# A graph layer's last group gets an order of its own: wide one-hots two groups sooner, the last quad in halves, normalizations in batches counted from the end

## The chip, the cores and the metric

The kernel runs on one core of one Trainium2 chip. The metric is the device time of the core in microseconds (us). Before the change it was 2016.4 us, the median of three runs (2014.7 to 2017.06). The engines have these short names: PE is TensorE (matmuls; PEld its weight loads), DVE is VectorE, ACT is ScalarE, POOL is GpSimd, and SP is SyncE, which only issues transfers here.

## What is computed

There are 6250 nodes with 128 features and 206250 edges, sorted by their receiver. Each edge gets a weight vector from two small networks, a score per head from the receiver's query, the sender's key and that weight, and adds score times the sender's value to its receiver. Each node's sum is added to its features and normalized.

```python
w  = silu(edge_feats @ rad_W1 + rad_b1) @ rad_W2 + rad_b2
w += silu(chi_scalar @ sph_W1 + sph_b1) @ sph_W2 + sph_b2
q_i = (x @ Wq)[receivers]; k_j = (x @ Wk)[senders]; v_j = (x @ Wv)[senders]
alpha = (q_i * w * k_j).sum per head / sqrt(16) * cutoff
out = segment_sum(alpha * v_j, receivers) / 16
return layernorm(x + out)          # per row, eps 1e-5
```

## The kernel before, in words

**Tiling.** 128 edges make a tile, four tiles a *quad* (512 edges), four quads a *group*. There are 403 quads in 101 groups; the last group, 100, has three. Inside a group the quads go in the order 0, 2, 1, 3, and the list `order` holds all of them. In this text "quad i" is the one at place i of `order`, so group g has quads 4g to 4g+3, and the last group's three are **a** (i = 400), **b** (401) and **c** (402).

**Start.** Keys and values of all nodes are computed and stored as a table in HBM, one row of 1 KB per node. The first ten quads are fed by gathers from `x` instead.

**Gathers.** The sender's rows come by `gathers`: four indirect transfers a quad, issued by POOL (the line of the helper is L125), one for each tile, into a ring of 16 buffers `kv`. They are issued 14 quads ahead, and each waits for a matmul of the quad that PE is at ("no gather ahead of TensorE"). Six quads (65, 130, ... 390) get their rows by 512 single transfers from SP instead (`load_rows`, buffers named `rows`, two of them). This stays as it is.

**A slot of the loop (L641 to L710).** In slot i PE makes the first layers of quad i+2 (L446), the queries at the edges of quad i+1 (`q_at_edges`, L457, into one of two PSUM buffers `pq`) and the second layer of quad i+1 (`weigh`, L488 and L493, into one of two buffers `pw`). ACT makes the two silus of quad i+2 (L478). DVE does `multiply(i+1)` (L500: query times key, which needs the gathered rows), then `scores(i)` (L507, L509, L511) and `messages(i)` (L522). PE later sums the messages of a group by one-hot matrices: `sum_quads` (L533), `part_sums` (ACT, L562), `sum_group` (PE, L567 and L569, which carries the group before along through a `to` matrix made by `place`, L556 and L557), and ACT copies the total (`tot`, L571). The engines work in the order of the program; waits on matmuls are put on certain instructions by hand (`after`, `behind`), so that a wait of DVE or ACT is for PE's current quad.

**The normalization (`statistics`, L573).** Two groups later, in the last slot of a group, DVE adds `x` to the total and takes mean and variance (L579 to L582). Every fourth group the batch is finished: one root on ACT (L585), a reciprocal and a shift on DVE (L587, L589), and the rows on ACT (L592). The batches are groups 0 to 3, 4 to 7, ..., 92 to 95; then 96 and 97 together, 98 alone, and 99 and 100 in the code behind the loop. Root and silu are of different tables on ACT, so that each such batch also has two table loads (rows `ACT_TABLE_LOAD`). The finished rows are written by SP (`write_rows`, L599), one group a slot. Where to is known only at run time, so each write waits for the one before it, and the very last one (L749) too.

**The last group.** It is summed by *wide* one-hots over 128 receivers (`wide_one_hots`, L537: three DVE instructions, the last of them 128x512) instead of `sum_quads`. Before, these lie in buffers of the silus (`act`) and are made in slots 399, 400 and 401. Behind the loop (L711 to L749) the last `sum_group`, the last quad's scores and messages in two halves, and the moments of groups 99 and 100 follow. A flag (`general`) that tells whether a slow general path is needed is loaded into registers of all engines at L696.

The lines at which the ends meet:

```python
messages(q, scores(q, halves[0]), halves[0])     # L729
...
moments(0, tot_of[g - 1])                        # L732: group 99
...
messages(q, alpha, halves[1])                    # L737
...
moments(1, po_of[g])                             # L744: group 100
...
nc.sync.dma_start(out[N - P:, :], y)             # L749
```

Of the kernel before, what the change touches and what calls it, by code (L numbers as in the profile page):

```python
# [24 lines left out]
P = 128  # L25
N = 6250
D = 128
# [31 lines left out]
def gnn_kernel(ctx, tc, x, src, dst, weight, edges, rad_W1, rad_b1, rad_W2, rad_b2,  # L59
# [344 lines left out]
    with tc.tile_pool(name="ps", bufs=1, space=PSUM) as pp:  # L404
# [93 lines left out]
        def multiply(q, mark=None):  # L498
            kq_of[q] = quad_of("kq", 3)
            o = nc.vector.tensor_tensor(kq_of[q], pq_of[q], kv_of[q][:, :, :D], op=OP.mult)  # L500
            if mark is not None:
                after(o, mark)
# [33 lines left out]

        def wide_one_hots(q):  # L537
# [5 lines left out]
            hot_of[q, "wide"] = ep.tile([P, EQ], F32, name="act", bufs=8).rearrange(  # L543
                "p (t r) -> p t r", r=P)
# [7 lines left out]
        def place(g):  # L552

            to = to_of[g] = gp.tile([P, 2, P], F32, name="to")
# [18 lines left out]
        def statistics(g):  # L573
            first = g // LB * LB if g < NG - 3 else g
# [3 lines left out]
            k = g - first + 1  # L578
            nc.vector.tensor_tensor(y0[:, k - 1, :], tot_of[g], x_of[g], op=OP.add)  # L579
            st = gp.tile([P, 6], F32, name="st")  # L580
            nc.vector.bn_stats(st, y0[:, k - 1, :])
            nc.vector.bn_aggr(mv[:, k - 1, :], st)  # L582
            if k == LB or g >= NG - 4:
                sd = gp.tile([P, LB], F32, name="sd")
                nc.scalar.activation(sd[:, :k], mv[:, :k, 1], AF.Sqrt, bias=eps)  # L585
                rs = gp.tile([P, LB], F32, name="rs")
                nc.vector.reciprocal(rs[:, :k], sd[:, :k])  # L587
                shift = gp.tile([P, LB], F32, name="shift")
                nc.vector.scalar_tensor_tensor(shift[:, :k], mv[:, :k, 0], -1.0, rs[:, :k],  # L589
                                               op0=OP.mult, op1=OP.mult)  # L590
                for i in range(k):
                    nc.scalar.activation(y0[:, i, :], y0[:, i, :], AF.Identity,  # L592
                                         scale=rs[:, i:i + 1], bias=shift[:, i:i + 1])
                    written.append((first + i, y0[:, i, :]))
# [46 lines left out]
        for g in range(NG):  # L641
            last = g == NG - 1
            for slot, j in enumerate((0, 2, 1, 3)):
                q = g * NQ + j
                i = g * NQ + slot
                if q >= QUADS:
                    continue
# [3 lines left out]
                if slot == 0 and g + 1 < NG:  # L651
# [3 lines left out]
                if slot == 2 and g + 1 < NG:  # L655
                    turned = make_q(g + 1)
                if 1 <= g:
                    for t in ((), (0, 1), (2, 3))[slot] if last else ((), (0, 1), (2,), (3,))[slot]:
                        mark = sum_quads(g - 1, t)
                if last and slot == 2:  # L660
                    po_of[g] = pp.tile([P, EQ], F32, name="ph", bufs=2)[:, :D]
                    for t in range(QT):
                        sum_wide(order[i - 2], t, start=(t == 0))
                if i + 2 < len(order):
                    first_layers(order[i + 2])
                if i + 1 < len(order):
                    mark = q_at_edges(order[i + 1])
                    marks = weigh(order[i + 1])
                if i + 2 < len(order):
                    silus(order[i + 2], mark, marks)  # L670
# [6 lines left out]
                if i + 1 < len(order):  # L677
                    multiply(order[i + 1], mark)
                    messages(q, scores(q, marks=marks), marks=marks)
# [6 lines left out]
                if slot == 1:  # L686
                    if g + 1 < NG:
# [220 lines left out]
```

## Time and profile before

| what | us |
|---|---|
| median of three runs | 2016.4 |
| the profiled execution's own time | 2016.52 |
| span of the profile (first to last instruction) | 2014.7 |
| busy in the span: PE, DVE, POOL, ACT | 1808.9, 1466.3, 1504.8, 720.1 |
| granted PE clock over the span | 0.92 |

The profiled execution took 2016.52 us, of which 1.8 us lie outside the span. Rows of the timeline give the start in us from the span's start, the duration in us, the engine, the line, the operation, what is written from what, and in brackets the idle time of the engine just before and what ended it. A row can stand for several instructions (the number behind x). Lines such as L500 are lines of the kernel before.

### The profile page before, as it was taken

The page shows a single profiled execution, that of the slowest core. Times are in us where ns is not written, and L with a number is a line of the kernel's source. Part 1 is how long each engine was busy: PE and PEld are TensorE (multiplying, and loading weights), DVE is VectorE, ACT ScalarE, POOL GpSimd, SP SyncE. Part 2 cuts the span into 40 slices and gives each one's busy share as a digit, 9 for nine tenths or more (in the row PEclk, how much of TensorE's full clock was granted, in tenths as well). Part 3 has the DMA queues.
Part 4 walks back from the last instruction along what each step waited for, and adds up shares of the span by engine and source line. Part 5 has one row for each costly group of instructions (what it writes and reads, how often), then busy time and mean ns, then how long its engine had stood idle before and what let it go on. Part 6 is the DMA issues. An engine that isn't in the chain of part 4 may idle for free.

```text
span 2014.7 us, 50499 instructions
## 1 busy us (share of the span) xinstructions
PE 1808.9 (90%) x16012; PEld 1515.0 (75%) x16012; DVE 1466.3 (73%) x3012; ACT 720.1 (36%) x1425; POOL 1504.8 (75%) x1596
## 2 busy tenths in 40 slices
PE   9898888999999988899999988988888999889987
PEld 7787777877887777777777777777777787777776
DVE  6687767878887867677767676777776777767776
ACT  2333333334433423333333233333333343332333
POOL 7777777777777777777777777777777777777774
PEclk9898988999998998998988888999998989899898
DMA  8454545555555555555454555454545555555552
GB/s 311 133 151 141 155 142 152 156 156 155 152 153 148 153 152 144 153 152 152 142 155 143 150 144 153 141 153 141 153 142 151 156 142 151 151 146 150 145 151 73
DMA packets 146414, 304.47 MB, mean 151 GB/s; under 512 B 36716, under 2 KB 79580, under 8 KB 146140
## 3 DMA queue, kind: packets, MB, share of 16 engines
q0 software_dynamic: 75584, 205.62, 36.4%
q1 hardware_dynamic: 69056, 95.15, 14.8%
q8 instruction: 128, 2.10, 0.4%
q14 instruction: 146, 1.20, 0.2%
q10 hardware_dynamic: 1500, 0.40, 0.1%
HBM read 287.58 MB, written 13.46 MB: 149 GB/s over the span
## 4 chain that ended last, share of the span: by engine, by line
PE 51%; DMA 21%; DVE 11%; issue 6%; ACT 4%; SPq 4%; POOL 3%; DVEq 0%; ACTq 0%; POOLq 0%
PE pw L493 25%; DMA kv<-kv_tab,src_i 17%; PE pq L457 10%; PE ph L446 7%; DVE kq L500 4%; PE po L533 3%; DMA feats<-in_edges 3%; SPq L167 3%; PE pw L488 2%; DVE kq L507 2%; DVE side L509 2%; POOL msg L125 2%; ACT y L592 1%; ACT L478 1%; POOL kv L125 1%
## 5 line engine op out<-in xcount | busy, mean ns | idle before, releaser
L125 POOL DMA_INDIRECT kv<-kv_tab,src_i x1548 | 1465.1, 946 | 474.3 <-PE pw L493 183.9
L478 ACT ACTIVATE act<-ph,b 128x512 f32<-128x512 f32 x806 | 518.2, 685 | 1159.8 <-PE pq L457 1126.5
L493 PE MATMUL pw<-w,act 128*128 128x128 f32 x6448 | 912.8, 300 | 0.0
L493 PEld LDWEIGHTS pw<-w,act 128*128 128x128 f32 x6448 | 831.6, 209 | 107.5 <-issue 95.9
L446 PE MATMUL ph<-feats,w 32*128 32x512 f32 x1612 | 495.2, 673 | 53.6 <-DMA feats<-in_edges 29.6
L457 PE MATMUL pq<-q,hotT 32*128 32x128 f32 x3224 | 498.1, 297 | 39.0 <-DVE kq L500 38.8
L500 DVE TENSOR_TENSOR kq<-pq,kv 128x512 f32<-128x512 f32 x397 | 273.1, 688 | 323.7 <-DMA kv<-kv_tab,src_i 169.3
L457 PEld LDWEIGHTS pq<-q,hotT 32*128 32x128 f32 x3224 | 418.6, 199 | 76.5 <-issue 45.1
L509 DVE TENSOR_REDUCE side<-kq 128x32 f32<-128x512 f32 x404 | 280.0, 693 | 42.3 <-PE pw L493 0.9
L522 DVE TENSOR_TENSOR msg<-kv,side 128x512 f32<-128x512 f32 x398 | 273.2, 686 | 44.0 <-DVE side L511 1.4
L507 DVE TENSOR_TENSOR kq<-pw,kq 128x512 f32<-128x512 f32 x404 | 274.2, 679 | 0.0
L446 PEld LDWEIGHTS ph<-feats,w 32*128 32x128 f32 x1612 | 135.5, 192 | 136.9 <-issue 90.3
L488 PE MATMUL pw<-brow,onesb 3*128 3x512 bf16 x403 | 161.6, 401 | 0.3 <-DVE kq L507 0.3
L533 PE MATMUL po<-msg,hot 128*32 128x128 f32 x3200 | 154.7, 290 | 0.0
L567 PE MATMUL pq<-part,to 128*128 128x128 f32 x200 | 45.2, 309 | 76.1 <-DVE kq L500 48.9
L511 DVE TENSOR_TENSOR side<-side,scale 128x32 f32<-128x32 f32 x404 | 80.6, 199 | 42.9 <-DVE side L509 0.9
L432 DVE TENSOR_TENSOR hotT<-relb,side 128x512 f32<-128x512 bf16 x101 | 68.8, 682 | 45.3 <-DMA relb<-rel_lin 45.3
L533 PEld LDWEIGHTS po<-msg,hot 128*32 128x32 f32 x3200 | 70.8, 111 | 39.0 <-issue 6.0
L567 PEld LDWEIGHTS pq<-part,to 128*128 128x128 f32 x200 | 31.3, 197 | 86.7 <-issue 53.8
L437 DVE TENSOR_TENSOR hot<-rel,side 128x512 f32<-128x512 f32 x100 | 66.1, 661 | 0.0
L426 PE MATMUL pq<-wq,xT 128*128 128x128 f32 (+1 forms) x202 | 46.8, 318 | 20.0 <-DVE kq L500 19.6
L426 PEld LDWEIGHTS pq<-wq,xT 128*128 128x128 f32 (+1 forms) x202 | 36.0, 223 | 24.6 <-DVE kq L500 23.8
(113 smaller groups left out, 839.3 us busy)
## 6 DMA issues: line engine op xcount, KB each, us to landing
feats<-in_edges SPq DMA_DIRECT2D x101, 512.0 KB
rows<-kv_tab SPq DMA_DIRECT2D x3072, 1.0 KB
kv<-kv_tab,src_i POOLq DMA_INDIRECT x1548
relb<-rel_lin SPq DMA_DIRECT2D x101, 128.0 KB
x<-in_x SPq DMA_DIRECT2D x101, 64.0 KB
out<-y SPq DMA_DIRECT2D x101, 64.0 KB
kv_tab<-kv SPq DMA_DIRECT2D x12, 512.0 KB
act<-in_x SPq DMA_DIRECT2D x12, 256.0 KB
```

The costliest lines, as they stand in the source:

```text
L125: return nc.gpsimd.indirect_dma_start(out=o, out_offset=None, in_=table, in_offset=bass.IndirectOffsetOnAxis(ap=index, axis=0))
L426: nc.tensor.matmul(pt[:n, :D], xT_of[g][:, :n], wq, start=True, stop=True)
L446: return nc.tensor.matmul(act_of[q, i], w1[r0:r0 + R, :], feats_of[g][r0:r0 + R, c0:c0 + EQ], start=True, stop=True)
L457: o = nc.tensor.matmul(pq_of[q][:, t, :], hotT_of[g][b, t * P:(t + 1) * P], q_of[g][b, :], start=True, stop=True)
L478: o = nc.scalar.activation(act, act_of[q, i], AF.Silu, bias=b1[:, i:i + 1])
L488: nc.tensor.matmul(pw, onesb, brow.rearrange("p t d -> p (t d)"), start=True, stop=False)
L493: o = nc.tensor.matmul(pw[:, t, :], act_of[q, i][:, t * P:(t + 1) * P], w2[:, i, :], start=False, stop=(t == QT - 1 and i == 1))
L500: o = nc.vector.tensor_tensor(kq_of[q], pq_of[q], kv_of[q][:, :, :D], op=OP.mult)
L507: nc.vector.tensor_tensor(m, pw_of[q][:, t, :], m, op=OP.mult)
L509: o = nc.vector.tensor_reduce(alpha, m.rearrange("p t (h e) -> p t h e", e=HD), AX.X, OP.add)
L522: o = nc.vector.tensor_tensor(msg_of[q][:, t, :].rearrange("p t (h e) -> p t h e", e=HD), kv_of[q][:, t, D:].rearrange("p t (h e) -> p t h ...
L533: o = nc.tensor.matmul(po_of[g][j * W:(j + 1) * W, :], hot_of[g][:, j * QT + t, :], msg_of[g * NQ + j][:, t, :], start=(t == 0), stop=(t = ...
```

## The change

It gives the last group an order written out by hand.

- **Loop.** It ends with group 99 (all conditions on the last group go away). The slots of groups 0 to 99 keep their instructions apart from what follows.
- **Wide one-hots.** They are made in slots 392 (a), 394 (b) and 396 (c) instead of 399, 400 and 401, and lie in the two buffers `rows` of the single transfers. `place(100)` goes to slot 398 (with a buffer of its own, `to_end`), `place(99)` to slot 399, the load of `general` from slot 401 to slot 396.
- **Batches of the normalization.** They are counted from the end: group 0 alone, then 1 to 4, ..., 93 to 96; the last batch is finished in slot 395. Groups 97, 98, 99 and 100 are normalized one by one. There are 29 roots instead of 28.
- **Behind the loop.** Silus of c before the root of group 97; `multiply(b)`; scores and messages of a; normalization of 97; then scores and messages of b; moments of 98; then `multiply`, scores and messages of c in two halves, with the normalization of 98 and the moments of 99 between the halves, and the normalization of 99 behind them; then the moments of group 100, its normalization on DVE and the last write.

The diff, cut to its core:

```diff
-        def multiply(q, mark=None):
-            kq_of[q] = quad_of("kq", 3)
-            o = nc.vector.tensor_tensor(kq_of[q], pq_of[q], kv_of[q][:, :, :D], op=OP.mult)
+        def multiply(q, mark=None, t=slice(0, QT)):
+            if t.start == 0:
+                kq_of[q] = quad_of("kq", 3)
+            o = nc.vector.tensor_tensor(kq_of[q][:, t, :], pq_of[q][:, t, :], kv_of[q][:, t, :D],
+                                        op=OP.mult)
...
-            hot_of[q, "wide"] = ep.tile([P, EQ], F32, name="act", bufs=8).rearrange(
-                "p (t r) -> p t r", r=P)
+            k = order[-3:].index(q)
+            if k % 2 == 0:
+                wides.append(quad_of("rows", 2, 2 * D).rearrange("p t (h r) -> p h t r", r=P))
+            hot_of[q, "wide"] = wides[-1][:, k % 2]
...
+        def first_of(g):
+            return max(g - (g - (NG - LB)) % LB, 0)
...
+        def statistics(g):
+            moments(g, tot_of[g])
+            if g < NG - LB and first_of(g + 1) > g:
+                normalize(first_of(g), g + 1, roots(first_of(g), g + 1))
...
-        for g in range(NG):
-            last = g == NG - 1
+        for g in range(NG - 1):
...
+                if g == NG - 3 and slot in (0, 2):
+                    wide_one_hots(order[slot // 2 - 3])
+                if g == NG - 2 and slot == 0:
+                    wide_one_hots(order[-1])
+                    n = nc.values_load(general, min_val=0, max_val=1)
+                if g == NG - 2 and slot == 2:
+                    place(NG - 1)
+                if g == NG - 2 and slot == 3:
+                    place(g)
+        g, (a, b, c) = NG - 1, order[-3:]
+        first_layers(c)
+        mark = q_at_edges(b)
+        marks = weigh(b)
+        turned = sum_group(g - 2)
+        for t in range(QT // 2):
+            sum_quads(g - 1, t)
+        silus(c, mark, marks)
+        sd = roots(g - 3, g - 2)
+        turned()
+        multiply(b, mark)
+        messages(a, scores(a, marks=marks), marks=marks)
+        normalize(g - 3, g - 2, sd)
+        write_rows()
+        mark = q_at_edges(c)
+        marks = weigh(c)
+        for t in range(QT // 2, QT):
+            sum_quads(g - 1, t)
+        po_of[g] = pp.tile([P, EQ], F32, name="ph", bufs=2)[:, :D]
+        for t in range(QT):
+            sum_wide(a, t, start=(t == 0))
+        part_sums(g - 1)
+        turned = sum_group(g - 1)
+        messages(b, scores(b, marks=marks), marks=marks)
+        moments(g - 2, tot_of[g - 2])
+        sd = roots(g - 2, g - 1)
+        turned()
+        for t in range(QT):
+            sum_wide(b, t)
+        nc.tensor.matmul(po_of[g], to_of[g][:, 1, :], tot_of[g - 1], start=False, stop=False)
+        multiply(c, mark, halves[0])
+        messages(c, scores(c, halves[0]), halves[0])
+        for t in range(QT // 2):
+            sum_wide(c, t)
+        normalize(g - 2, g - 1, sd)
+        write_rows()
+        moments(g - 1, tot_of[g - 1])
+        sd = roots(g - 1, g)
+        multiply(c, mark, halves[1])
+        messages(c, scores(c, halves[1]), halves[1])
+        for t in range(QT // 2, QT):
+            sum_wide(c, t, stop=(t == QT - 1))
+        normalize(g - 1, g, sd)
+        write_rows()
+        moments(g, po_of[g])
+        sd = roots(g, g + 1)
...
         nc.sync.dma_start(out[N - P:, :], y)
```

`roots` and `normalize` are the two halves of what `statistics` did at the end of a batch: the root on ACT, and reciprocal, shift and rows.

More of the change, by code (lines that the diff above doesn't have):

```diff
@@ L577, in statistics @@
             y0, mv = y0_of[first]
-            k = g - first + 1
-            nc.vector.tensor_tensor(y0[:, k - 1, :], tot_of[g], x_of[g], op=OP.add)
+            k = g - first
+            nc.vector.tensor_tensor(y0[:, k, :], total, x_of[g], op=OP.add)
             st = gp.tile([P, 6], F32, name="st")
[L581 to L594, printed above, removed]
+            nc.vector.bn_stats(st, y0[:, k, :])
@@ L650, in gnn_kernel @@
                     verdict()
-                if slot == 0 and g + 1 < NG:
+                if slot == 0:
                     turned = turn_q(g + 1)
```

106 lines of the change are left out of this document (42 added, 64 removed).

## The prediction

> **What bounds the kernel now.** I read the groups of instructions first, then the waits of POOL, then POOL's timeline.
>
> ```profile
> span 2014.7 us, 50499 instructions
> ...
> PE 1808.9 (90%) x16012; PEld 1515.0 (75%) x16012; DVE 1466.3 (73%) x3012; ACT 720.1 (36%) x1425; POOL 1504.8 (75%) x1596
> ...
> L125 POOL DMA_INDIRECT kv<-kv_tab,src_i x1548 | 1465.1, 946 | 474.3 <-PE pw L493 183.9
> ```
>
> ```profile
> POOL kv L125 <- PE pw L493: 183.9, 595, 2.8
> ```
>
> ```profile
> 53.84 0.95 POOL L125 DMA_INDIRECT kv<-kv_tab,src_i  x1 [0.31 <-issue]
> ...
> 77.09 0.95 POOL L125 DMA_INDIRECT kv<-kv_tab,src_i  x1 [2.79 <-PE pw L493]
> ```
>
> ```profile
> 1987.09 0.95 POOL L125 DMA_INDIRECT kv<-kv_tab,src_i  x1 [0.30 <-issue]
> ...
> 1992.08 0.95 POOL L125 DMA_INDIRECT kv<-kv_tab,src_i  x1 [0.30 <-issue]
> ```
>
> POOL looks 75% busy and PE 90%, yet POOL is the bound. 1548 gathers of 0.946 us, with 474.3/1548 = 0.306 us ahead of each, make a period of 1.25 us; 1548 x 1.252 is 1938 us, and from the first row (53.84) to the end of the last (1993.03) there are 1939 us. The waits put down to PE are 183.9/595 = 0.309 us each, the same 0.3 us that stands ahead of every gather, so this is POOL's own gap and no wait. One wait was real, the longest: 2.79 us at 77.09. A quad's four gathers take 5.00 us, and the last gathers of b and c start at 1987.09 and 1992.08. Nothing that the change does on other engines shortens this chain. What it can change is the tail: 2014.7 - 1993.0 = 21.7 us behind the last gather, and how soon the other engines are ready for it.
>
> **The tail before.** DVE, then PE and ACT, then SP's queue:
>
> ```profile
> 1985.32 0.69 DVE L500 TENSOR_TENSOR kq<-pq,kv 128x512 f32<-128x512 f32 x1 [1.15 <-DMA kv<-kv_tab,src_i]
> ...
> 1989.61 0.17 DVE L587 RECIPROCAL rs<-sd 128x2 f32<-128x2 f32 x1 [0.36 <-ACT sd L585]
> ...
> 1989.89 0.16 DVE L541 CAST d<-dst_i 128x4 f32<-128x4 int32 x1
> ...
> 1991.24 0.69 DVE L500 TENSOR_TENSOR kq<-pq,kv 128x512 f32<-128x512 f32 x1
> 1991.85 0.68 DVE L507 TENSOR_TENSOR kq<-pw,kq 128x512 f32<-128x512 f32 x1
> ...
> 1994.34 0.16 DVE L541 CAST d<-dst_i 128x4 f32<-128x4 int32 x1
> ...
> 1995.93 0.68 DVE L500 TENSOR_TENSOR kq<-pq,kv 128x512 f32<-128x512 f32 x1
> ...
> 2001.81 0.42 DVE L507 TENSOR_TENSOR kq<-pw,kq 128x256 f32<-128x256 f32 x1
> 2002.26 0.43 DVE L509 TENSOR_REDUCE side<-kq 128x16 f32<-128x256 f32 x1
> ...
> 2002.94 0.42 DVE L522 TENSOR_TENSOR msg<-kv,side 128x256 f32<-128x256 f32 x1
> 2004.26 0.29 DVE L722 TENSOR_TENSOR y<-tot,x 128x128 f32<-128x128 f32 x1 [0.90 <-ACT tot L571]
> ...
> 2005.01 0.39 DVE L507 TENSOR_TENSOR kq<-pw,kq 128x256 f32<-128x256 f32 x1
> ...
> 2006.25 0.42 DVE L522 TENSOR_TENSOR msg<-kv,side 128x256 f32<-128x256 f32 x1
> ...
> 2008.87 0.34 DVE L747 TENSOR_SCALAR y<-y,mv,rs 128x128 f32<-128x128 f32 x1
> ```
>
> ```profile
> 1991.99 1.43 PE L457 MATMUL pq<-q,hotT 32*128 32x128 f32 x5 [1.94 <-DVE kq L500]
> ...
> 1998.71 1.21 PE L549 MATMUL ph<-msg,act 128*128 128x128 f32 x8
> 2002.63 0.80 PE L567 MATMUL pq<-part,to 128*128 128x128 f32 x2 [2.71 <-ACT part L562]
> ```
>
> ```profile
> 1990.01 0.88 ACT L592 ACTIVATE y<-y,shift,rs 128x128 f32<-128x128 f32 x2 [0.43 <-DVE shift L589]
> ...
> 2003.95 0.28 ACT L571 ACTIVATE tot<-pq 128x128 f32<-128x128 f32 x1 [1.37 <-PE pq L569]
> ...
> 2006.42 0.49 ACT L740 ACTIVATE y<-y,shift,rs 128x128 f32<-128x128 f32 x1 [0.94 <-DVE shift L735]
> ```
>
> ```profile
> 2006.94 0.33 SPq L599 DMA_DIRECT2D out<-y  x1
> 2010.18 0.34 SPq L749 DMA_DIRECT2D out<-y  x1
> ```
>
> ```profile
> SPq L599 <- DMA out<-y: 4.1, 3, 1.9
> ...
> SPq L749 <- DMA out<-y: 2.8, 1, 2.8
> ```
>
> DVE does kq of a, b and c at 1985.32, 1991.24 and 1995.93. From kq of b to the last messages (2006.25) it needs 15.01 us, in which it also makes the wide one-hots of b and c and waits 0.90 us for the total of group 99. Two things set the end. DVE finishes the last row at 2008.87 + 0.34 = 2009.21, but SP issues the last write only at 2010.18: it waits 2.8 us for the write of group 99, issued at 2006.94, to land. So the end hangs on group 99's rows (2006.42 on ACT), which hang on DVE's queue.
>
> **The change, part by part.** The loop's slots keep their instructions, so POOL's 1548 gathers and the place of the last one stay: cost nothing, by the saturated period above.
>
> *Wide one-hots, `place`, `general` earlier.* About 1.6 us of DVE (1994.34 to 1995.93 holds one quad's wide one-hot and a `place`) go from each of the slots 399 to 401 into 392 to 398, where DVE waits for gathers and PE. There they lie under waits like the 1.15 us at 1985.32; if that cover is gone, 1.6 us are late in one slot. The buffers `rows` were last read in slot 390 by DVE itself, so nothing waits for them. The load of `general` stands in PE's queue behind the second layer of quad 397:
>
> ```profile
> L696 PEldq TENSOR_LOAD <-general x1: 491/491/491, 1994.0 to 1994.0; - x1
> ```
>
> Here it ran at 1994.0, while matmuls already issued kept PE busy (the windows below show PE busy all 3.40 us from 1992.0): nothing, and 0.5 us in one slot if PE has nothing in hand.
>
> *The batch 93 to 96 in slot 395.* Before, a batch of four ended in slot 391, and this is what followed:
>
> ```profile
> 1957.60 0.69 DVE L500 TENSOR_TENSOR kq<-pq,kv 128x512 f32<-128x512 f32 x1 [2.91 <-PE pq L457]
> ...
> 1963.10 0.69 DVE L500 TENSOR_TENSOR kq<-pq,kv 128x512 f32<-128x512 f32 x1 [1.04 <-PE pq L457]
> ...
> 1971.12 0.68 DVE L500 TENSOR_TENSOR kq<-pq,kv 128x512 f32<-128x512 f32 x1
> ```
>
> These are the kq of quads 394, 395 and 397. Last gathers start 5.00 us apart back from 1987.09 (quad 401), so theirs at 1952.1, 1957.1 and 1967.1. So kq lies 5.5, 6.0 and 4.0 us behind the gather, against 3.23 us where DVE waits for the landing (quad 400: 1985.32, its gather at 1982.09). DVE waits for PE (the brackets), since root, rows and table loads hold up the silus that PE needs, and six quads behind the batch it is not all made up. In the changed kernel the same comes four slots later: kq of b, six behind the batch, lies between 1987.09 + 3.23 = 1990.32 (all made up) and 1987.09 + 4.04 = 1991.13. No row is nearer, so I take the middle, **1990.7**, 0.5 us sooner than before. This part gives back most of what the empty slots would give. What goes for it is the batch of 96 and 97 in slot 399, whose rows (1990.01) held up c's silus.
>
> *The new order of DVE from kq of b.* By start-to-start times: kq 0.61 (1991.24 to 1991.85); scores and messages of a 2.49 (to 1994.34); reciprocal and shift of 97 0.28 (1989.61 to 1989.89); scores and messages of b 2.49; moments of 98 0.75 (2004.26 to 2005.01); c's first half: kq, which no row shows in this shape, between 0.39 (L507 at half size) and 0.61 (full), taken as 0.45 like the half at 2001.81, then 1.13 (2001.81 to 2002.94) and messages 0.42, together 2.00; reciprocal and shift of 98 0.28; moments of 99 0.75; second half up to its messages 0.45 + 1.13 = 1.58. The sum is **11.23 us** instead of 15.01. The last messages start at 1990.7 + 11.2 = 2001.9, 4.3 us sooner. c's gathers land by 1995.3 (1992.08 + 3.23), when DVE is at a's or b's scores: no wait. Halving `multiply` costs 0.3 us of DVE and hides nothing here.
>
> *Behind it.* From the last messages to DVE's last row before: 2009.21 - 2006.25 = 2.96 us, so 2004.9. Group 99's rows: messages 0.42, reciprocal to row 0.40 (1989.61 to 1990.01), row 0.49, issue 0.03: 2003.3, which is 1.4 us behind the last messages where it was 0.7 before. Its landing took 3.24 us from issue to the next issue (2006.94 to 2010.18), and earlier ones up to 0.34 + 1.9 + 0.04 = 2.3. Between these I take 2.8, the middle. The last write then goes out at **2006.1** instead of 2010.18: 4.1 us gained. The end still hangs on group 99's write and not on DVE. What follows the last write (4.5 us) stays.
>
> **Sum.** The profiled execution's 2016.52 becomes 2012.4; against the median of 2016.4 I forecast **2012.3 us**.
>
> **A rule and a row: the PE clock.**
>
> ```profile
> 1988.60:1992.00 3.40, 1.46 (x25) 1.07 (x24) 2.86 (x10) 2.27 (x4) 2.57 (x3) 1.00 0.48 127
> 1992.00:1995.40 3.40, 3.40 (x15) 3.18 (x16) 3.02 (x7) 2.90 (x5) 0.95 (x1) 0.50 0.39 109
> ```
>
> The first column after the stretch is its length, then busy PE, PEld, DVE, ACT and POOL, then the granted clock. PE was busy 1.46 of 3.4 us, its longest gap 1.94 us (ended at 1991.99), and the clock then was 0.50. The Trainium skill, "TensorE: Matmul & The Clock Gate", section "What's actually happening", has the clock halved after an idle window of some 3.4 us; by that rule the tail, with no such gap, keeps the full clock. The trace halves it after less, so the rule is too mild here, and the half clock is a rival. In my forecast PE has work up to kq of b, because the batch at 395 leaves it late, and PE lies beside DVE.
>
> **The rivals.**
>
> 1. *Half clock in the tail.* PE needs 7.93 us at half clock from c's queries to the end of a's wide sum (1991.99 to 1998.71 + 1.21), and 1.6 us from `sum_group` to the copied total (2002.63 to 2003.95 + 0.28). From kq of b's end (1991.4) that gives 2000.9 for group 99's total, while DVE wants it at 1990.7 + 8.9 = 1999.6. DVE then waits 1.3 us: gain 2.8, **2013.6 us**. For it: the two rows above. Against it: PE's gap before 1991.99 came from DVE's one-hots and roots, which are gone.
> 2. *All made up, quick landing.* kq of b at 1990.32 and 2.3 us for the write: 0.9 us more, **2011.4 us**. For it: the wide one-hots are out of slots 399 to 401. Against: the row at 1971.12.
> 3. *It doesn't do what it says*: the lateness behind the batch grows with the one-hots in slots 392 to 396, kq of b comes at 1994 or later, and the gain is under 1 us: **2015.5 us**. Against: 5.00 us a quad leave DVE over 1 us free (the waits above).
> 4. *Slower.* Group 0 as a batch of its own adds one more root and two table loads in slot 11, in the stretch in which PE is behind POOL. POOL may then wait for PE's marks, and every such us moves the last gather.
>
> ```profile
> 118.41 2.05 PE L493 MATMUL pw<-w,act 128*128 128x128 f32 x16
> ```
>
> ```profile
> 135.88 0.95 POOL L125 DMA_INDIRECT kv<-kv_tab,src_i  x1 [0.30 <-PE pw L493]
> ```
>
> The first row is the second layer of quad 12 (ends 120.5), for which quad 26's first gather, next after the second row, waits (137.1): 16.7 us to spare. A batch cost some 2.8 us above (6.0 against 3.23). It decides from 16.7 us on, and the kernel is slower if it costs 25: then 2016.4 + 4.2 = **2020.6 us**. Against it: the factor of nine.
>
> **How the numbers follow.** Chances: forecast 0.60 (its own range 2011.3 to 2013.2), half clock 0.20, quick 0.12, no gain 0.05, slower 0.03. 0.2% of 2016.4 is 4.0 us, about what a measurement of this kernel can tell from no change, so 2012.4 divides faster from same; the forecast lies on that line. Of its 0.60 a little over half, 0.35, is below. Faster 0.35 + 0.12 = 0.47; same 0.25 + 0.20 + 0.05 = 0.50; slower 0.03. The range runs from the quick case less the 1 us by which the runs before scatter (2010.4) to the half-clock case plus that (2014.6).
>
> **What would show it.** Last gather still at about 1992; kq of b at 1990.3 to 1991.1, waiting for a landing or for nothing; DVE without a gap from there to the last messages, 11.2 us later; no DVE wait for `tot`; the last write held by group 99's write, at 2005.2 to 2007. Wrong would be: a last gather later than 1994, kq of b after 1992, a DVE wait of over 1 us behind kq of b, or a last write that DVE and not SP's wait releases.

## The result, and the profile after

The changed kernel takes 2010.88 us (median of 8 runs, 2009.01 to 2011.89), the kernel before 2016.73 us (8 runs, 2014.7 to 2018.14). The ratio is 0.9972 with an interval of [0.9961, 0.9983], so 3.4 to 7.9 us are gained. The forecast was 2012.3 us. The profiled execution took 2011.89 us, the longest of its eight, 4.63 less than that of before. Line numbers from here on are those of the changed kernel (`multiply` L501, `scores` L509 to L513, `messages` L524, moments L590 to L593, rows L612, writes L624, last write L778).

The page of the changed kernel, first its span, then busy times, then the gathers with their mean in ns and the idle time ahead of them:

```profile
span 2010.1 us, 50508 instructions
...
PE 1811.3 (90%) x16012; PEld 1519.6 (76%) x16012; DVE 1466.5 (73%) x3015; ACT 720.8 (36%) x1426; POOL 1505.3 (75%) x1596
...
L125 POOL DMA_INDIRECT kv<-kv_tab,src_i x1548 | 1465.3, 947 | 474.3 <-PE pw L493 186.0
```

Nothing has moved here. The same 1548 gathers are busy for 1465.3 us instead of 1465.1, with the same 474.3 us between them. Their timeline:

```profile
54.44 0.95 POOL L125 DMA_INDIRECT kv<-kv_tab,src_i  x1 [0.30 <-DVE kv L260]
...
77.60 0.94 POOL L125 DMA_INDIRECT kv<-kv_tab,src_i  x1 [2.78 <-PE pw L493]
...
1992.76 0.95 POOL L125 DMA_INDIRECT kv<-kv_tab,src_i  x1 [0.30 <-issue]
```

The one real wait of POOL, 2.78 us early on, was there before. The last gather starts at 1992.76, 0.68 us later than before (1992.08), of which 0.6 us were already there at the first (54.44 against 53.84). So the gain lies behind the last gather, and there DVE's queue shows it:

```profile
1991.45 0.69 DVE L501 TENSOR_TENSOR kq<-pq,kv 128x512 f32<-128x512 f32 x1
...
1998.06 0.41 DVE L501 TENSOR_TENSOR kq<-pq,kv 128x256 f32<-128x256 f32 x1
...
2001.07 0.40 DVE L501 TENSOR_TENSOR kq<-pq,kv 128x256 f32<-128x256 f32 x1
...
2002.64 0.42 DVE L524 TENSOR_TENSOR msg<-kv,side 128x256 f32<-128x256 f32 x1
...
2004.37 0.29 DVE L590 TENSOR_TENSOR y<-ph,x 128x128 f32<-128x128 f32 x1 [1.05 <-PE ph L555]
...
2005.83 0.34 DVE L777 TENSOR_SCALAR y<-y,mv,rs 128x128 f32<-128x128 f32 x1
```

No row from kq of b (1991.45) to the last messages (2002.64) has a bracket, those left out here included: DVE waits for nothing there, neither for the gathers of c nor for a total. Only behind them does it wait, 1.05 us for PE. On ACT and in SP's queue the end looks like this:

```profile
2003.36 0.49 ACT L612 ACTIVATE y<-y,shift,rs 128x128 f32<-128x128 f32 x1 [1.83 <-DVE shift L608]
```

```profile
2003.88 0.33 SPq L624 DMA_DIRECT2D out<-y  x1
2006.29 0.34 SPq L778 DMA_DIRECT2D out<-y  x1
```

```profile
SPq L778 <- DMA out<-y: 2.0, 1, 2.0
```

Group 99's rows are written at 2003.88, and the last write goes out at 2006.29, when that write has landed. SP waited 2.0 us for it. The last row of DVE was done at 2005.83 + 0.34 = 2006.17, so the two are only 0.12 us apart now, where before DVE was done 0.97 us ahead of the last write.

In a table, each step against the one ahead of it (us; the forecast's column is worked out from its own numbers):

| step | before | after | difference | forecast |
|---|---|---|---|---|
| last gather starts | 1992.08 | 1992.76 | +0.68 | 0 |
| kq of b against that | -0.84 | -1.31 | -0.47 | -0.54 |
| kq of b to last messages | 15.01 | 11.19 | -3.82 | -3.78 |
| last messages to group 99's write | 0.69 | 1.24 | +0.55 | +0.65 |
| that write to the last write | 3.24 | 2.41 | -0.83 | -0.44 |
| last write to the end of the span | 4.49 | 3.82 | -0.66 | 0 |
| sum | | | -4.55 | -4.11 |

### The profile page after: what moved, and what is told of

Read it like the earlier page. It is cut to its first block, busy times and chain, and to the rows that moved or that the text cites. A ratio compares the mean times of both kernels' runs of the same rounds, so it can differ in the third digit from the quotient of the medians.

```text
span 2010.1 us, 50508 instructions
## 1 busy us (share of the span) xinstructions
PE 1811.3 (90%) x16012; PEld 1519.6 (76%) x16012; DVE 1466.5 (73%) x3015; ACT 720.8 (36%) x1426; POOL 1505.3 (75%) x1596
## 4 chain that ended last, share of the span: by engine, by line
PE 53%; DMA 20%; DVE 11%; issue 6%; ACT 4%; POOL 3%; SPq 2%; DVEq 0%; ACTq 0%; POOLq 0%
PE pw L493 27%; DMA kv<-kv_tab,src_i 17%; PE pq L457 10%; PE ph L446 7%; DVE kq L501 4%; PE po L535 4%; PE pw L488 2%; DMA feats<-in_edges 2%; DVE side L511 2%; DVE kq L509 2%; POOL msg L125 2%; POOL kv L125 1%; SPq L167 1%; ACT L478 1%; ACT y L612 1%
## 5 line engine op out<-in xcount | busy, mean ns | idle before, releaser
L125 POOL DMA_INDIRECT kv<-kv_tab,src_i x1548 | 1465.3, 947 | 474.3 <-PE pw L493 186.0
L446 PE MATMUL ph<-feats,w 32*128 32x512 f32 x1612 | 497.2, 676 | 41.0 <-ACT act L478 20.9
L501 DVE TENSOR_TENSOR kq<-pq,kv 128x512 f32<-128x512 f32 x398 | 273.4, 687 | 331.9 <-DMA kv<-kv_tab,src_i 188.2
L524 DVE TENSOR_TENSOR msg<-kv,side 128x512 f32<-128x512 f32 x398 | 273.2, 686 | 43.2 <-PE pq L457 0.9
L509 DVE TENSOR_TENSOR kq<-pw,kq 128x512 f32<-128x512 f32 x404 | 274.5, 679 | 0.1
L446 PEld LDWEIGHTS ph<-feats,w 32*128 32x128 f32 x1612 | 136.9, 193 | 123.8 <-issue 80.0
L513 DVE TENSOR_TENSOR side<-side,scale 128x32 f32<-128x32 f32 x404 | 80.6, 200 | 42.6 <-DVE side L511 0.5
L125 POOL DMA_INDIRECT msg<-in_x,src_x x40 | 39.0, 976 | 13.5 <-issue 11.6
```

Of the source, the lines that this page charges most:

```text
L125: return nc.gpsimd.indirect_dma_start(out=o, out_offset=None, in_=table, in_offset=bass.IndirectOffsetOnAxis(ap=index, axis=0))
L446: return nc.tensor.matmul(act_of[q, i], w1[r0:r0 + R, :], feats_of[g][r0:r0 + R, c0:c0 + EQ], start=True, stop=True)
L501: o = nc.vector.tensor_tensor(kq_of[q][:, t, :], pq_of[q][:, t, :], kv_of[q][:, t, :D], op=OP.mult)
L509: nc.vector.tensor_tensor(m, pw_of[q][:, t, :], m, op=OP.mult)
L513: o = nc.vector.tensor_tensor(alpha, alpha, scale[:, q * QT + t.start:q * QT + t.stop, None].to_broadcast([P, n, HEADS]), op=OP.mult)
L524: o = nc.vector.tensor_tensor(msg_of[q][:, t, :].rearrange("p t (h e) -> p t h e", e=HD), kv_of[q][:, t, D:].rearrange("p t (h e) -> p t h ...
```

## The experiments

The theory: POOL's gathers, at 1.25 us without a gap, set when the last quad's rows are there, and only what DVE's queue holds behind kq of b, and then group 99's write, decides the rest. The rivals are in the expectations. There is one profile of each kernel. Since the place of the last gather differs by some us from run to run (last section), the profiles are compared by their *tail*, the time from the start of the last gather to the end of the span: 22.59 us before, 17.36 after. E1 to E4 ran beside the kernel before at a median of 2015.73 us (30 runs), F1 to F4 beside it at 2017.24 us (27 runs). All ratios are against the kernel before.

### E1: the kernel before with the early wide one-hots alone

The one-hots, `place` and the flag are moved as in the change; the order behind the loop and the batches stay.

```diff
-                        wide_one_hots(g * NQ + 1)
-                        place(g)
...
+                if g == NG - 3 and slot in (0, 2):
+                    wide_one_hots(order[slot // 2 - 3])
+                if g == NG - 2 and slot == 0:
+                    wide_one_hots(order[-1])
...
+                if g == NG - 2 and slot == 2:
+                    place(NG - 1)
```

> The kernel before with one part alone: the wide one-hots, the places 99 and 100 and the load of the flag in slots 392 to 399, in the buffers of single rows. Chain theory (the end is DVE's queue behind the last gathers, then group 99's write): kq of b 0.9 us sooner (1990.3), kq of c no sooner than its landing (1995.3, 0.6 us sooner) with b's scores still queued behind it, and 1.3 us less between b's messages and the moments of 98: 1.9 us gained, 2014.8. Rival, the one-hots are the whole gain and the order nothing: 5 us or more, 2011.7 or less. Rival, one-hots lay under waits all along: no gain, 2016.7.

Measured: 2012.66 us (11 runs), ratio 0.9985 [0.9976, 0.9994]; tail 18.48 us. The last messages come 11.56 us behind the last gather, against 14.17 before and 9.88 after. DVE in the tail:

```profile
1997.92 0.69 DVE L500 TENSOR_TENSOR kq<-pq,kv 128x512 f32<-128x512 f32 x1 [1.54 <-PE pw L493]
...
2006.44 0.41 DVE L522 TENSOR_TENSOR msg<-kv,side 128x256 f32<-128x256 f32 x1
```

The first row is kq of c. DVE now stands idle for 1.54 us ahead of it, and it starts 3.04 us behind c's last gather (1994.88), near the 3.23 us at which the kernel before began a quad whose landing it waited for. The bracket names PE's second layer, since its signal came last (1997.86 in the trace); but the signals of c's last landing go on to 1997.80, so the landing alone would have held the row about as long. b's scores are queued behind it. So the early one-hots alone gain 2.6 us up to the last messages, and some of the time that they free turns into a wait at the head of the queue. What follows: in the profile the one-hots are the larger part and not the whole. The times alone can't tell this: the interval of E1 holds the 1.9 us expected and overlaps with the change's own.

### E2: the changed kernel with the one-hots made late

```diff
-                if g == NG - 3 and slot in (0, 2):
-                    wide_one_hots(order[slot // 2 - 3])
...
+        wide_one_hots(b)
+        place(g - 1)
...
+        wide_one_hots(c)
+        place(g)
```

> The changed kernel with that part alone undone: one-hot of a in slot 399, of b and c behind the scores of a and b, with the places. Chain theory: kq of b 0.5 us later, then 1.6 us (b and place) and 1.3 us (c and place) more in DVE's queue: 3.4 us lost, 2014.3. Rival, the new order alone brings the gain: 2010.9. Rival, one-hots are all: 2016 or more.

Measured: 2015.68 us (11 runs), ratio 0.9996 [0.9987, 1.0005]; tail 20.74 us, 3.4 more than after. DVE:

```profile
1995.71 0.69 DVE L551 TENSOR_TENSOR rows<-d,side 128x512 f32<-128x512 f32 x1
...
2000.06 0.69 DVE L551 TENSOR_TENSOR rows<-d,side 128x512 f32<-128x512 f32 x1
...
2006.25 0.42 DVE L524 TENSOR_TENSOR msg<-kv,side 128x256 f32<-128x256 f32 x1
```

The two one-hots stand between the messages again, and the last messages come 12.43 us behind the last gather (1993.82), 2.55 later than after; 0.70 us more of the 3.4 lie behind the last write (4.52 against 3.82). E1 and E2 agree from both sides: of the 4.29 us by which the last messages come sooner (14.17 to 9.88), about 2.6 are the one-hots and about 1.7 the new order. This holds where kq of b lies in each profile, 4.16 us behind its gather before, 3.34 in E1, 3.33 in E2 (where 0.5 us later than after was expected) and 3.70 after. Counted from kq of b, DVE's queue up to the last messages is 15.01 us before, 14.11 with the order alone (E2), 13.24 with the one-hots alone (E1) and 11.19 with both: alone the parts take out 0.90 and 1.77 us, together 3.82, more than their sum. The change without its early one-hots can't be told from no change by its time.

### E3: the last quad multiplied whole

```diff
-        multiply(c, mark, halves[0])
+        multiply(c, mark)
...
-        multiply(c, mark, halves[1])
```

> The changed kernel with c's multiply in one piece ahead of the first half. Chain theory: c's rows have landed (1996.0) when DVE gets there (1998.1), so the halves only cost 0.44 + 0.43 - 0.61 = 0.3 us: 0.2 to 0.3 us gained, 2010.6, and no DVE wait for a landing. Rival, the halves hide c's landing: a DVE wait for the landing and up to 1 us lost, 2011.9.

Measured: 2010.84 us (10 runs), ratio 0.9975 [0.9966, 0.9985]; tail 16.13 us. One row in the place of the two halves at 1998.06 and 2001.07, without a wait:

```profile
2000.81 0.69 DVE L501 TENSOR_TENSOR kq<-pq,kv 128x512 f32<-128x512 f32 x1
```

From kq of b to the last messages there are 11.09 us instead of 11.19, so the halves cost 0.1 us and hide no landing. That is below what the times can tell.

### E4: the last full batch ends at group 95, as before the change

Group 96 is then normalized together with 97 behind the loop.

```diff
-            return max(g - (g - (NG - LB)) % LB, 0)
+            return g // LB * LB if g < NG - 1 else NG - 1 - LB
...
-            if g < NG - LB and first_of(g + 1) > g:
+            if g < NG - 1 - LB and first_of(g + 1) > g:
...
-        sd = roots(g - 3, g - 2)
+        sd = roots(g - 4, g - 2)
```

> The changed kernel with batches of the normalization ending at 95 (slot 391, as before the change) and group 96 finished together with 97 behind the loop: no root, rows and table loads in slot 395. Chain theory: PE has made up when the tail begins, kq of b 3.2 to 3.3 us behind its last gather instead of 3.70, so 0.4 to 0.5 us gained, 2010.4. Rival, the batch in 395 costs the tail nothing: 2010.9. Rival, half clock: with PE no longer late it idles before the tail, the clock halves in it and DVE waits for the total of 99: 0.5 to 1.3 us lost, 2011.4 to 2012.2.

Measured: 2010.36 us (9 runs), ratio 0.9976 [0.9966, 0.9986]; tail 16.53 us. DVE, PE, and then the stretches with length, busy PE, PEld, DVE, ACT and POOL, and the granted clock:

```profile
1990.51 0.69 DVE L501 TENSOR_TENSOR kq<-pq,kv 128x512 f32<-128x512 f32 x1 [1.06 <-DMA kv<-kv_tab,src_i]
```

```profile
1991.25 0.82 PE L457 MATMUL pq<-q,hotT 32*128 32x128 f32 x5 [1.50 <-DVE kq L501]
```

```profile
1987.60:1991.00 3.40, 2.15 (x31) 1.76 (x29) 2.27 (x7) 2.10 (x4) 2.48 (x4) 1.00 0.40 111
1991.00:1994.40 3.40, 3.15 (x22) 3.03 (x23) 3.05 (x8) 0.40 (x2) 1.70 (x2) 0.83 0.41 116
1994.40:1997.80 3.40, 3.40 (x33) 2.76 (x32) 2.92 (x9) 1.05 (x4) 0.00 (x0) 0.67 0.14 39
```

With the batch four quads further off, all is made up by kq of b: it waits for its landing and starts 3.45 us behind its last gather (1987.06), 0.25 us sooner than after (3.70). That can't be put down to the batch, though: E2 and E3, and F3 below, have the batch where the change has it, and their kq of b waits for its landing too (0.41, 0.78 and 0.68 us) and starts 3.31 to 3.33 us behind its gather. PE idles 1.50 us here, and its clock is 0.50 from 1993.26 to 1996.68, which the last two stretches share (0.83 and 0.67); DVE still waits for nothing up to the last messages. Neither shows in the time. Where the batch ends is worth a few tenths of a us at most.

### F1 and F2: seven and five quads through SP

```diff
-ROW_QUADS = 6
+ROW_QUADS = 7
```

> The changed kernel with seven quads instead of six whose rows come as single transfers from SP, so that POOL has four gathers less; in the session in which every kernel took some 2635 us it could not speak on POOL, so it is run again. Theory (at the usual speed POOL's gathers, 1.25 us each without a gap, set the whole length, and the tail hangs behind the last gather): the last gather is 4 x 1.25 = 5.0 us sooner, the tail as in the changed kernel, 2010.9 - 5.0 = 2005.9 us. Rival (SP's single transfers or PE are about as late as POOL): the last gather is less than 2 us sooner, or POOL waits for PE, 2009 us or more.

Measured with seven: 2064.85 us (5 runs), ratio 1.0236 [1.0217, 1.0255]. The groups of `L446` (first layers of PE) with seven quads, and in the changed kernel:

```profile
L446 PE MATMUL ph<-feats,w 32*128 32x512 f32 x1612 | 516.2, 697 | 226.6 <-DMA feats<-in_edges 200.5
```

```profile
L446 PE MATMUL ph<-feats,w 32*128 32x512 f32 x1612 | 497.2, 676 | 41.0 <-ACT act L478 20.9
```

PE now waits 200.5 us for the edges' features, which the kernel loads through the same queue of SP as the single rows. A stretch of SP's queue with seven quads:

```profile
1200.05 10.75 SPq L167 DMA_DIRECT2D rows<-kv_tab  x28
1210.90 0.37 SPq L172 DMA_DIRECT2D feats<-in_edges  x1
```

28 single rows hold SP for 10.75 us, and the features are issued behind them; PE then waits 4.51 us for these, up to 1214.6. POOL, with four gathers less, is not even sooner (its last gather starts at 1997.99), since it waited for PE on the way (once 5.26 us, at 334.55), and the tail behind it is 60.4 us long. The theory's 5 us didn't come. The rival held, far beyond the size that it gave: with a seventh quad PE waits for what stands in SP's queue, and POOL is no longer the bound. That queue is not full even then (SP waits 77.6 us in all for its own writes to land); what comes late is what stands behind the rows.

> The changed kernel with five quads instead of six whose rows come as single transfers from SP, so that POOL has four gathers more; run again as well. Theory (POOL's gathers set the length): 5.0 us longer, 2015.9 us, tail behind the last gather unchanged. Rival (the single transfers take up time of the DMA engines or of SP that the gathers want, as fewer of them made the kernel faster in the 2635 us session): same or faster than 2010.9 us.

Measured with five: 2018.9 us (11 runs), ratio 1.0011 [1.0002, 1.0020], some 7 us more than the change's ratio makes of the same 2017.24 (0.9972 x 2017.24 = 2011.6). Its gathers:

```profile
L125 POOL DMA_INDIRECT kv<-kv_tab,src_i x1552 | 1468.5, 946 | 475.5 <-PE pw L493 185.1
```

Four gathers more and 1468.5 + 475.5 = 1944.0 us instead of 1939.6, with no new wait: 4.4 us of the 5.0 expected. The tail is 20.06 us, 2.7 us longer than after, as kq of b lies 6.6 us behind its gather instead of 3.7. The edit does one thing more, which may well be behind this: the places of these quads are spread anew, and the last of them is quad 395 instead of 390. POOL skips such a quad, and so is some 5.0 us ahead from there (an estimate, from the four gathers of a quad). Behind quad 390 the changed kernel's DVE next waits for a landing five quads later (1961.92); here the last quad of rows is multiplied at 1968.68, only six quads ahead of b, and no wait for a landing follows. So 4.4 us are POOL's, and for the 2.7 of the tail the shifted quad is the likely reason; no run moved that quad alone. POOL's bound holds downward, and of five, six and seven quads six is the best.

### F3: PE kept busy ahead of the last messages

```diff
+        idle = pp.tile([P, D], F32, name="po")
+        for _ in range(8):
+            nc.tensor.transpose(idle, ident, ident)
```

> The changed kernel with eight idle transposes on PE behind the first half of c's wide sum, so that PE is not idle ahead of the last messages. Theory (the write of group 99 holds the last write; the half clock of PE behind the last messages costs DVE only about 0.5 us that the write hides): DVE's last row comes some 0.5 us sooner behind the last messages (3.0 instead of 3.5 us), the last write at most 0.1 us sooner, time 2010.8 us, within 0.2 us of the changed kernel. Rival (DVE's last row holds the last write): 0.4 to 0.5 us sooner, 2010.4 us.

Measured: 2012.61 us (11 runs), ratio 0.9978 [0.9969, 0.9987], inside the interval of the change's own. DVE and SP:

```profile
2003.12 0.42 DVE L524 TENSOR_TENSOR msg<-kv,side 128x256 f32<-128x256 f32 x1
...
2004.34 0.29 DVE L590 TENSOR_TENSOR y<-ph,x 128x128 f32<-128x128 f32 x1 [0.54 <-PE ph L555]
...
2005.80 0.34 DVE L780 TENSOR_SCALAR y<-y,mv,rs 128x128 f32<-128x128 f32 x1
```

```profile
2004.36 0.33 SPq L624 DMA_DIRECT2D out<-y  x1
2006.89 0.34 SPq L781 DMA_DIRECT2D out<-y  x1
```

DVE waits 0.54 us for PE instead of 1.05, and its last row ends 3.02 us behind the last messages (after: 3.53). E3 and E4 have the same 0.53 and 0.54 us and end as soon without any transposes, so that this is not the transposes' doing for certain (point 5 below). The last write is not sooner for it: 3.77 us behind the last messages, after 3.65. It goes out 0.75 us after the last row is done, so it waits for group 99's write, as the theory has it.

### F4: together, with group 99's rows ahead of c's last messages

E3, E4 and F3 in one, and this:

```diff
-        messages(c, scores(c, halves[1]), halves[1])
+        alpha = scores(c, halves[1])
+        normalize(g - 1, g, sd)
+        write_rows()
+        messages(c, alpha, halves[1])
...
-        normalize(g - 1, g, sd)
-        write_rows()
```

> Batches of the normalization end at group 95 again (group 96 is done together with 97 behind the loop), multiply of c is whole, eight idle transposes keep PE busy ahead of the last messages, and the reciprocal, shift and row of group 99 come before c's last messages instead of behind them. Theory (tail hangs on kq of b, then DVE's queue, then group 99's write, then DVE's last row): the write of group 99 goes out 0.4 us or more ahead of where it was, DVE's last row some 0.5 us sooner behind the last messages, last write 0.9 to 1.2 us sooner behind the last gather than in the changed kernel, 2009.8 us. Rival (the end is set elsewhere): 2010.3 us or more, as the batch to 95 alone (2010.36).

Measured: 2013.48 us (11 runs), ratio 0.9983 [0.9974, 0.9992]; tail 18.20 us, 0.84 longer than after. DVE and SP:

```profile
2004.59 0.34 DVE L782 TENSOR_SCALAR y<-y,mv,rs 128x128 f32<-128x128 f32 x1
```

```profile
2002.55 0.33 SPq L626 DMA_DIRECT2D out<-y  x1
2005.80 0.35 SPq L783 DMA_DIRECT2D out<-y  x1
```

```profile
SPq L783 <- DMA out<-y: 2.8, 1, 2.8
```

Against the last gather (1992.15), group 99's write goes out at 10.40 us instead of 11.12 and the last row ends at 12.78 instead of 13.41: both sooner, as expected. The last write goes out at 13.65, 0.1 later than after: the write ahead of it took 3.25 us where it took 2.41. So the expected 0.9 to 1.2 us didn't come and the rival's time did; the step up to the write was right, and what undid it is the landing, which the last section takes up. No kernel here beats the changed one: the ratios of E3, E4, F3 and F4 all overlap with its interval.

### Runs that speak of other things

F1 to F4 had been run once before, in a session in which every kernel, the one before too, took some 2635 us. Against its 2635.67 us there (24 runs), seven quads took 2647.01 (1.0037 [1.0023, 1.0052]), five 2615.55 (0.9912 [0.9897, 0.9928]), the busy PE 2634.45 (0.9994 [0.9982, 1.0005]) and all together 2632.85 (0.9978 [0.9968, 0.9989]). What had been expected of them there:

> The changed kernel with seven quads' rows from SP instead of six: four gathers fewer on POOL. Theory that POOL's gathers bound everything up to the tail: the last gather starts 4 x 1.25 = 5.0 us sooner and the tail behind it stays at 17.4 us: 2005.9. Rival, PE (90% busy) is the bound: the last gather is sooner but the tail grows by as much: 2010.9. Rival, SP cannot issue the rows in time: slower than 2010.9, with DVE waiting for rows.

> The changed kernel with five quads' rows from SP: four gathers more on POOL. Theory that POOL's gathers bound everything: 5.0 us later, 2015.9, the tail as it is. Rival, PE is the bound: 2010.9, with a shorter tail.

> The changed kernel with eight idle transposes on PE between the sums of c's two halves (their result is not used), where PE waited 2.23 us and the granted clock fell to 0.5 after. If that wait halves the clock: the last sum takes 0.7 us instead of 1.2 and DVE's last row comes 0.5 us sooner behind the last messages (3.0 instead of 3.5 us). Write theory (the last write waits for group 99's): the time falls by at most 0.2 us, 2010.7. Rival, DVE's last row sets the end: 0.5 us, 2010.4.

> Together: batches to 95, c's multiply whole, eight idle transposes, and the reciprocal, shift and row of group 99 ahead of c's last messages instead of behind. Theory: 0.25 us from kq of b, 0.3 from the whole multiply, group 99's write 0.65 us sooner against the last messages, which come 0.3 us later, and the last row 0.5 us sooner by the clock: the last write 0.9 to 1.2 us sooner behind the last gather (12.4 instead of 13.5 us), 2009.8. Rival, some other queue holds the last write: 2010.4 as with the batches alone.

The gathers and what PE waited for in the third of them:

```profile
L125 POOL DMA_INDIRECT kv<-kv_tab,src_i x1548 | 1462.8, 945 | 1047.9 <-PE pw L493 437.4
```

```profile
PE pq L426 <- issue: 170.4, 71, 3.8
PE ph L446 <- issue: 127.8, 120, 4.7
```

POOL idles 1047.9 us ahead of its gathers instead of 474.3, and PE waits hundreds of us for nothing that the profile shows. POOL was not the bound there, so these runs could not test the theory. What held PE up, and why one quad less through SP gains 20 us there, stays open. In the tail the busy PE did there as in F3: last messages to last row 3.03 us; but so did five quads without it, with 3.03 as well.

## Why the prediction was right, point by point

1. *POOL bounds the kernel and nothing in the change touches it.* Shown. The gathers take the same time before and after (1465.1 and 1465.3 us, with 474.3 between), and four more of them cost 4.4 us in POOL's own queue (F2). That the fourth rival (one root more in slot 11 holds POOL up) was wrong is seen in the one real wait, 2.78 us as before. What the prediction left out: SP's queue can't carry a seventh quad in time (F1), so this bound could not have been pushed further by more rows through SP.
2. *kq of b between 3.23 and 4.04 us behind its gather, taken at 3.6.* It was 3.70, and that this is so near the middle is luck. The lateness behind the batch is there: DVE waits 1.65, 1.39 and 0.16 us for PE ahead of quads 398, 399 and 400. But in E2, E3 and F3, with the same batch, it is made up by kq of b, which waits for its landing at 3.31 to 3.33 us, near the lower bound. The last gathers came 0.84 to 3.2 us later in these three than after, which gave the other engines that much more time. So no run shows the batch to set kq of b; it hangs on where POOL stands.
3. *From kq of b to the last messages 11.23 us.* It was 11.19, without a gap. With the one-hots of b and c put back (E2) the same stretch takes 14.11, 2.92 us more, where the expectation had 1.6 + 1.3 = 2.9. What the prediction did not say, E1 shows: without the new order, part of what the one-hots free is spent in a 1.54 us wait of kq of c for its landing, with b's scores behind it.
4. *Halving costs 0.3 us and hides nothing.* It hides nothing; the size was 0.1 us (E3).
5. *Last messages to the last row 2.96 us.* This term was too small for this profile: it was 3.53. PE's clock was halved around the last messages, as the windows and PE's queue of the changed kernel show:

```profile
1988.60:1992.00 3.40, 3.40 (x33) 2.99 (x32) 3.09 (x9) 1.64 (x3) 2.49 (x4) 1.00 0.38 99
...
1999.40:2002.80 3.40, 0.98 (x7) 0.60 (x5) 3.09 (x13) 0.79 (x2) 0.00 (x0) 1.00 0.07 19
2002.80:2006.20 3.40, 1.22 (x4) 0.93 (x4) 1.77 (x8) 0.79 (x2) 0.00 (x0) 0.51 0.09 24
```

```profile
2000.18 0.71 PE L555 MATMUL ph<-msg,rows 128*128 128x128 f32 x4 [0.51 <-DVE msg L524]
2003.12 1.22 PE L555 MATMUL ph<-msg,rows 128*128 128x128 f32 x4 [2.23 <-DVE msg L524]
```

   Around kq of b PE was busy throughout and had the full clock, as the forecast said; the half-clock rival placed the drop there and was wrong in that. In E4 and F4 the drop did come there, for one stretch of 3.41 us (0.50 from 1993.26 and 1992.68 on), and DVE did not wait for group 99's total in either, so a drop there does not by itself bring the rival's 1.3 us. In the changed kernel the drop came 11 us later than kq of b: PE was busy 0.98 of 3.40 us, with gaps up to 2.23 us, and the same four matmuls took 1.22 us instead of 0.71. The Trainium skill's rule (TensorE: Matmul & The Clock Gate, "What's actually happening"), an idle window of some 3.4 us, would have kept the clock full here too; the trace has it halved after a window that was 29% busy.

   The gap alone does not decide it. E4 and F1 have the same gap ahead of the same four matmuls and no transposes in it, and the clock stays full; first E4, then F1:

```profile
2002.19 0.71 PE L555 MATMUL ph<-msg,rows 128*128 128x128 f32 x4 [2.23 <-DVE msg L524]
```

```profile
2051.86 0.71 PE L555 MATMUL ph<-msg,rows 128*128 128x128 f32 x4 [2.23 <-DVE msg L524]
```

   In the changed kernel the clock falls at 2002.87, 0.25 us ahead of the four; in E4 it falls at 2003.50 and in F1 at 2053.65, behind them. Within each trace the changes of the clock lie whole steps of 3.41 us apart (after: 1972.15, 1982.39 and 2002.87, that is 3 and 6 steps), so that the 0.5 us hang on where such a step falls. The changed kernel, E2 and F2 are hit, E1 in part; E3, E4, F1, F3 and F4 are not. F3's own step falls at 2005.36, so its 0.5 us may be its place and not its transposes. What F3 does show is that the 0.5 us cost nothing at the end: the last write waits for group 99's write all the same. The forecast had the two in this order, so that the error in this term did not reach the end.

6. *Group 99's write is out 1.4 us behind the last messages and takes 2.8.* It was 1.24 and 2.41, the latter near the lower of the two bounds (2.3). The middle was a poor choice: at the usual speed the step took 2.40 to 2.60 us or 2.99 to 3.25, and nothing between (last section).
7. *What follows the last write stays 4.5 us.* It was 3.82. This term was carried over without a bound; in nine profiles it was 3.03 to 4.73, and the last section argues for the same cause as for term 6.
8. *The time.* The gain up to the last write was forecast as 4.1 us and measured 4.57 against the last gather; the whole, 4.11 forecast, was 4.55 in the profiles. That these are so near is luck in part: a last gather 0.68 us later hides most of the 0.39 and 0.66 us by which terms 6 and 7 were better than forecast. The medians differ by 5.85 us, 1.3 more than the profiles, and no profile shows where those lie. The interval of 3.4 to 7.9 us holds the forecast and also 4.0 us, at which the forecast divided faster from same, so that the runs do not settle that choice.

## What to carry to other kernels

When one engine's queue is full from beginning to end, a change elsewhere is worth what it does to the tail behind that queue's last instruction; list the tail's chain with start-to-start times, and compare profiles from that last instruction on, not from the beginning. Work that does not depend on the last data goes ahead of it, and the instructions that wait for that data go behind those that need nothing more: without the second, the first turns in part into waiting at the head of the queue (E1). Shifting load from the full queue to another one pays only until that one holds other work up, and that can be the very next step (F1: +2.4%).

## What the runs showed of the hardware that was not expected

**The next write follows a write of 64 KB after 2.4 or after 3.2 us, and a fetch of instructions goes with the difference.** These are the transfers around the last write, in slices of 0.075 us: before (from 2010.2, the write issued at 2010.18), then after (from 2006.3, issued at 2006.29).

```profile
DMA  0000000000058949000300000000004101000000
...
q1 hardware_dynamic: 144, 0.07, 8.1%
q8 instruction: 1, 0.02, 2.3%
```

```profile
DMA  0000200400058941100500000000000000000000
...
q1 hardware_dynamic: 144, 0.07, 8.3%
q14 instruction: 3, 0.02, 3.0%
```

Both writes have 144 packets that move about 0.85 us behind the issue. Before, 9 of them move only in the slices from 2012.46 on, after the one packet of queue q8, a fetch of 16 KB of instructions (1.09 us, from 2011.38 to 2012.47), has ended; after, no such fetch lies there (the three packets of q14 are fetches of 8 KB, and nothing is late beside them), and all 144 are through by 2007.85. The last two writes of nine profiles (before, after, E1 to E4, F2, F3, F4) agree with it. Eight of these eighteen had 9 packets, as many as are one of 16 DMA engines' share of 144, 0.65 us or more behind all others, each directly behind the end of such a fetch. Wherever that was group 99's write, the last write followed 2.99 to 3.25 us later, otherwise 2.40 to 2.54; wherever it was the last write, the span ended 4.49 to 4.73 us behind it, otherwise 3.03 to 3.82. Where the fetch ended sooner, the delay was smaller: with seven quads the 9 packets were 0.27 us behind the others and the step took 2.60 us; with seven quads in the 2635 us session it was 0.40 us and 2.74. Which write is hit differs among kernels, and may differ among runs; no run here moved a fetch on purpose, so that the fetch is the cause is argued from this agreement.

**The place of the last gather differs by up to 4 us from profile to profile.** In the eight profiles with 1548 gathers at the usual speed, the last gather starts between 1992.06 (E4) and 1995.94 (E3). The groups of these two:

```profile
L125 POOL DMA_INDIRECT kv<-kv_tab,src_i x1548 | 1469.2, 949 | 474.0 <-issue 187.9
```

```profile
L125 POOL DMA_INDIRECT kv<-kv_tab,src_i x1548 | 1464.8, 946 | 474.3 <-PE pw L493 185.7
```

3 ns a gather are 4.4 us of busy time over the kernel, nearly as much as the whole change gains. E1 has 949 ns too, and the other six have 946 or 947; nothing in the edits touches the gathers. In E2 and F3 another thing moves the last gather: the one early wait for PE takes 4.57 and 3.76 us there instead of 2.78. The profiled runs of E1 and E3 are the slowest of their kernels (2015.13 and 2013.83 us, medians 2012.66 and 2010.84), which fits; but with one profile of each kernel, that the scatter of the runs comes from POOL is argued and not shown.
